# The first MLP product of a vision tower by seven quarter products, with ScalarE's copies placed anew

## The chip, the cores and the metric

The kernel runs on one core of one Trainium2 chip. The metric is the device time in microseconds of one execution; lower is better. All matrix products are in float32.

## What is computed

The reference is one tokenizer, one attention-like layer and one layer of eight experts. Cut to what matters:

```
h = (rfft of overlapping patches of x) @ tok_W.T              # 16384 tokens of 256
n = layernorm(layernorm(h)) * ln1_g + ln1_b
q, k, v = n @ Wq.T + bq, n @ Wk.T + bk, n @ Wv.T + bv
mem[t] = decay * mem[t-1] + k[t] * v[t]                       # along time
x = layernorm(h) + q * mem
h2 = layernorm(x) * ln2_g + ln2_b
a = relu(h2 @ W1.T + b1)                                      # 256 -> 1024: the first MLP product
h = h + x + (a @ W2.T + b2)                                   # 1024 -> 256
t = layernorm(h);  choose the top 2 of 8 experts from t @ router_w.T
out = h + t + sum over the two of weight * (gelu(t @ w1[e] + b1[e]) @ w2[e] + b2[e])
```

## The kernel before, in words

**Blocks.** The 16384 tokens are worked in 32 blocks of 512 (`NB`, `BLK`). A block lives in a `Block` object whose methods issue the steps. The main loop runs over `i` from 0 to 30 and works on three blocks in each turn: `new` (block i: embedding, norm, q/k/v, scan, residual), `mid` (block i-1: the MLP) and `old` (block i-2: routing and sending its rows to the experts). Between them lie the experts' tiles: 256 rows of one expert each, about four in a block, done by `Tile` objects. After the loop a tail finishes the last block and the tiles left.

**Order.** PE, ACT, DVE and SP run under a schedule written out by hand (`manual_schedule`): each of these queues holds its instructions in the order in which the Python code issues them, and an instruction whose input isn't there holds up all behind it. Many methods are generators, and a `next(...)` issues the part up to the next `yield`. Only GpSimd's (POOL's) queue is ordered by the framework.

**One turn, in the order of issue.** (1) `embed` (L383 on): 20 products of 256 columns in three parts. ScalarE copies the first two results to `ab` (L405); VectorE forms the tile rows `h` from `ab` and from PSUM (L402, L422) and their statistics (L263, L264); GpSimd raises them to a power (`Norm.factors`, L283 to L288); VectorE writes the normed rows `zz` (L292). (2) Between the parts of `embed`: `features2` of `mid`, four ScalarE copies that put the transposed rows together as `hT` (L332), and `rows` and `turn3` of `old` (L698 and a DMA transpose). (3) `sum_up` (L620, L621): `h` plus `z`, plus the offsets `b2` of the second MLP product. (4) A slot for one expert tile (`expert_halves`): ScalarE's two copies to `xT` (L995), TensorE's `enter` (L1002) with Gelu (L1010), and `leave` of the tile before it (L1019), then VectorE's `sums` (L1031 to L1038) and GpSimd's adds to the output (L1048). (5) The first MLP product, `mlp_in`, in eight parts m of 128 output features: TensorE in `feature_mm` (L339), then a Relu on ScalarE (L640). In between, at m = 1, `join3` (four ScalarE copies to `tokT`, L332) and `split1` (two ScalarE copies to `planes`, L318, and a DMA transpose of them to `turned`, L326); at m = 3 a second tile; at m = 4 `store`, four ScalarE operations (L683) and a DMA; at m = 5 the first half of `differences` for the next block, `features1` (four VectorE copies, L332) and `mix_tokens` (L508 to L511). (6) `logits` (L723) and `choose` (L747 on). (7) The q, k and v products, each already by seven products of quarters (`products`, L524 to L560): the 256 features and the 512 tokens are each cut in two. One of each pair of left-hand quarters is replaced by a sum prepared once (`wqkv_mix`), one of each pair of right-hand quarters by a sum made on the block (`s1`, `s2`, `s4`). Two more tiles stand between its rounds. (8) `scan` (L586 to L597), the second MLP product's first half (`mlp_out(0)`, L650, added to `h` at L657), `residual` (transposes at L608, added at L611, statistics, `factors_here`), `split2` (as `split1`, of the second norm, for `features2` of the next turn), and `mlp_out(1)` with `take`, a row of small VectorE operations that assigns the next tiles.

**Buffers that matter.** PSUM: three `tm` buffers in turn (embedding, `leave`, `mlp_out`, `residual`, `logits`), two `mm` buffers (`enter`, q/k/v), and three fixed banks `sums`. SBUF: one `turned`, one `planes`, five buffers for expert weights (641.5 KB each), six for a tile's rows `xh`, two `xT`.

The first six blocks (`EARLY`) turn their rows on TensorE instead of by DMA. The change adds `run` ahead of `Turn` and leaves the rest of what isn't shown below as it is.

Of the kernel before, what the change touches and what calls it, by code (L numbers as in the profile page):

```python
# [36 lines left out]
def vit_tower_kernel(  # L37
# [120 lines left out]
    nc.sync.dma_start(out=w1_sb, in_=w1.rearrange("(k p) h -> p k h", p=P))  # L158
    w2_sb = const.tile([P, KH, D], F32)
# [26 lines left out]
    for e in range(E + 1):  # L186
# [13 lines left out]
    none = const.tile([P, 2, RW], F32)  # L200
    nc.gpsimd.memset(none, 0.0)
    nc.gpsimd.iota(
        none[:, :, NUMBER : NUMBER + 1].bitcast(I32), pattern=[[1, 2]], base=NTOK, channel_multiplier=2
    )

# [5 lines left out]
    six = ctx.enter_context(tc.tile_pool(name="six", bufs=6))  # L211
    five = ctx.enter_context(tc.tile_pool(name="five", bufs=5))
    twelve = ctx.enter_context(tc.tile_pool(name="twelve", bufs=12))
    small = ctx.enter_context(tc.tile_pool(name="small", bufs=2))

# [25 lines left out]
    def mix_weights():  # L241

        w = wqkv_sb.rearrange("p w k (m q) -> p w k m q", q=P)
        t1, t2, t4 = [wqkv_mix[:, :, i, :] for i in range(3)]
        nc.vector.tensor_tensor(t1, w[:, :, 0, 1], w[:, :, 0, 0], ALU.subtract)
        nc.vector.tensor_tensor(t2, w[:, :, 1, 1], t1, ALU.subtract)
        nc.vector.tensor_tensor(t4, w[:, :, 1, 0], t2, ALU.subtract)
        nc.vector.tensor_tensor(w[:, :, 0, 1], w[:, :, 1, 1], w[:, :, 0, 1], ALU.subtract)

    def restore_weights():  # L250

        w = wqkv_sb.rearrange("p w k (m q) -> p w k m q", q=P)
        nc.vector.tensor_tensor(w[:, :, 0, 1], w[:, :, 1, 1], w[:, :, 0, 1], ALU.subtract)
# [57 lines left out]

    class Turn:


        def split(self, src):
            planes = one.tile([P, TT, 2 * D], U16, name="planes")
            for i, half in enumerate(halves(src)):
                nc.scalar.copy(planes[:, :, i * D : (i + 1) * D], half)  # L318
            self.start([planes.rearrange("p t d -> p (t d)")])

        def start(self, planes):
            self.turned = one.tile([P, TT, 2, KD, P], U16, name="turned")
# [5 lines left out]
        def join(self, dst, copy):  # L328
            for k in range(KD):
                to = dst[:, k, :].bitcast(U16).rearrange("p (t q i) -> p i t q", t=TT, i=2)  # L330
                for i in range(2):
                    copy(to[:, 1 - i], self.turned[:, :, i, k, :])  # L332

# [16 lines left out]
    class Block:  # L350
# [83 lines left out]

        def first_norm(self):
# [10 lines left out]
        def split1(self):  # L446
# [3 lines left out]
            self.turn.split(self.zz)  # L450
# [52 lines left out]
        def mix_tokens(self):  # L503

            room = one.tile([P, TT, 2 * D], U16, name="planes").rearrange("p t d -> p (t d)").bitcast(F32)
# [113 lines left out]
        def sum_up(self):  # L619
            nc.vector.tensor_tensor(self.h, self.h, self.z, ALU.add)  # L620
            nc.vector.tensor_tensor(self.h, self.h, mb2_sb.unsqueeze(1).to_broadcast([P, TT, D]), ALU.add)  # L621
# [7 lines left out]
        def features2(self):  # L629
# [4 lines left out]
            self.turn.join(self.hT, nc.scalar.copy)  # L634

# [74 lines left out]
        def join3(self, copy):  # L710
            self.tokT = one.tile([P, KD, BLK], F32, name="tokT")
            self.turn.join(self.tokT, copy)
# [19 lines left out]
        def choose(self):  # L732
# [7 lines left out]
            lg = small.tile(shape, F32, name="lg")  # L740
# [5 lines left out]
            turned = small.tile([P, TT, G], F32, name="turned_lg")  # L746
# [3 lines left out]
            key = small.tile(shape, F32, name="key")  # L750
# [40 lines left out]
        def place(self, at_once=True):  # L791
# [5 lines left out]
            before = small.tile([P, TT, E], F32, name="before")  # L797
# [153 lines left out]
    added = []  # L951

    class Tile:
# [6 lines left out]
        def load(self):  # L960
            t = self.t
            self.w = five.tile([P, NW], F32, name="w")
            if self.block.i < NS - 1:
                wrow = nc.sync.value_load(self.table[:, 0, t : t + 1], min_val=0, max_val=(E - 1) * P)
                nc.sync.dma_start(out=self.w, in_=wex[bass.ds(wrow, P), :])
# [5 lines left out]
            self.xh = six.tile([P, 2 * KD, S], U16, name="xh")  # L971
# [9 lines left out]

        def fetch(self):
            if self.block.i >= NS - 1:

# [73 lines left out]
    class Expert:  # L1058
# [10 lines left out]

        def fetch(self):  # L1070
            pass
# [51 lines left out]
    at = dict(load=0, fetch=0, turn=0, enter=0, leave=0, sums=0)  # L1123
# [8 lines left out]
    def expert_halves(fetch=True, sums=True, load=True, turn=True):  # L1132

        n = at["enter"]
        if load:
            advance("load", n + AHEAD)
        assert at["load"] >= min(n + 2, len(tiles))
        advance("turn", n + 1 + turn)
        advance("enter", n + 1)
        yield  # L1140
# [5 lines left out]

    def run(steps):
        for _ in steps:
            pass
# [8 lines left out]
    def slot_halves(known, load=True, sums=True):  # L1158

        if len(tiles) - at["enter"] > LEFT and at["enter"] + 2 <= known:  # L1160
            yield from expert_halves(load=load, sums=sums)

    def slot(known, load=True):
        run(slot_halves(known, load))
# [7 lines left out]
    with tc.manual_schedule(engines=MANUAL):  # L1172
# [3 lines left out]
        for i in range(NS):  # L1176
# [3 lines left out]
            old = blocks[i - 2] if i >= 2 else None  # L1180
            embed = new.embed()
            next(embed)
            if i > 1:
                mid.features2()
# [15 lines left out]
            if at["enter"]:  # L1200
                slot(known, load=False)
            for m in range(KH):
                if mid:
                    mid.mlp_in(m)
                if m == 1:
                    if old and i >= EARLY:
# [3 lines left out]
                    if at["enter"]:  # L1210
                        advance("load", at["enter"] + AHEAD - 1)
# [4 lines left out]
                if m == KH // 2 and old:  # L1216
                    if i < EARLY:
                        old.join3(nc.scalar.copy)
                    old.store()
# [241 lines left out]
```

## Time and profile before

| what | value |
|---|---|
| median of 3 runs | 2113.02 us (2112.82 to 2114.13) |
| the profiled execution, its own time | 2116.49 us |
| its span, first to last instruction | 2114.7 us |
| mean granted TensorE clock | 0.994 |
| embedding of block 7 starts / of the last block | 370.07 / 1853.01 us |
| first MLP product, 32 blocks (L339) | 451.7 us busy, x1024 instructions |
| ScalarE's Relu behind it (L640) | 167.0 us busy, x256 |

From 370.07 to 1853.01 the loop runs 24 blocks in 1482.9 us, 61.8 each. A float32 product is two instructions on TensorE in the trace.

A line of the page or of a list of groups names source line, engine, operation and tiles; then come the count and busy time. In a timeline a line begins with the start and the duration in us of a run of like instructions; a bracket at its end says how long the engine had idled before it, and for what. "PEld" is TensorE's weight load, "SPq" SP's queue.

### The profile page before, as it was taken

To read this page: it belongs to the slowest core of one execution; us is meant where nothing else is said; L and a number is where in the kernel's file an instruction comes from. 1 tells how busy PE (TensorE), PEld (TensorE's weight loads), DVE (VectorE), ACT (ScalarE), POOL (GpSimd) and SP (SyncE) were. 2 spreads that over 40 slices of the span, in tenths; PEclk is the share of its full clock that TensorE was granted. 3 is DMA by queue.
4 is the path that set the end of the run, shared out by engine and by line. 5 is a ranking of instruction groups with operands and counts; after the bars stand their busy time and mean duration, and the time that the engine had idled before them with its cause. 6 is when DMAs were issued, how large, how long until landed. Compare 5 with 4: busy or idle time off the path is not lost.

```text
span 2114.7 us, 30454 instructions
## 1 busy us (share of the span) xinstructions
PE 2077.4 (98%) x9042; PEld 1576.0 (75%) x9042; DVE 1674.8 (79%) x5179; ACT 1100.8 (52%) x1966; POOL 886.9 (42%) x768
## 2 busy tenths in 40 slices
PE   8999999999999999999999999999999999998999
PEld 5777677777777777777777777787777787676776
DVE  6778888888888888888888888888888888767445
ACT  2344455655545565554556555455665545543453
POOL 1032234444444444544444444444444444535444
PEclk9999999999999999999999999999999999999999
DMA  4031256766676676567667766766776567688653
GB/s 142 4 123 64 80 131 138 160 143 129 134 157 146 155 160 139 125 143 159 156 143 160 150 122 136 157 156 143 163 157 118 138 149 161 138 197 168 91 69 50
DMA packets 424519, 283.21 MB, mean 134 GB/s; under 512 B 355104, under 2 KB 391072, under 8 KB 420256
## 3 DMA queue, kind: packets, MB, share of 16 engines
q1 hardware_dynamic: 373424, 208.35, 42.5%
q0 software_dynamic: 49632, 67.39, 17.8%
q10 hardware_dynamic: 1296, 5.52, 0.8%
q8 instruction: 71, 1.16, 0.2%
q14 instruction: 96, 0.79, 0.1%
HBM read 118.36 MB, written 86.52 MB: 97 GB/s over the span
## 4 chain that ended last, share of the span: by engine, by line
PE 74%; DVE 11%; ACT 5%; DMA 5%; issue 2%; POOL 2%; SPq 1%; another core or an unknown queue 0%; ACTq 0%; DVEq 0%; POOLq 0%
PE tm L650 17%; PE sums L339 13%; PE tm L396 9%; PE sums L524 9%; PE mm L1002 8%; PE tm L1019 8%; DMA turned<-planes 3%; DVE st L263 2%; PE mm L540 1%; ACT planes L318 1%; ACT tokT L332 1%; PE tm L1098 1%; PE mm L1081 1%; PE mm L539 1%; SPq L326 1%
## 5 line engine op out<-in xcount | busy, mean ns | idle before, releaser
L1048 POOL DMA_INDIRECT out<-y,xg x226 | 369.2, 1634 | 432.7 <-DVE y L1038 220.2
L650 PE MATMUL tm<-w_sb,aT 128*128 128x256 f32 x2048 | 454.7, 380 | 0.0
L339 PE MATMUL sums<-hT,w_sb 128*128 128x512 f32 x1024 | 451.7, 593 | 1.3 <-ACT aT L640 1.3
L650 PEld LDWEIGHTS tm<-w_sb,aT 128*128 128x128 f32 x2048 | 386.7, 190 | 57.2 <-DVE z L611 4.8
L819 POOL DMA_INDIRECT xbuf<-row,to x248 | 257.1, 1037 | 294.3 <-DVE ks L560 170.5
L339 PEld LDWEIGHTS sums<-hT,w_sb 128*128 128x128 f32 x1024 | 193.4, 190 | 219.9 <-issue 201.0
L396 PE MATMUL tm<-wu,xv 128*128 128x256 f32 x1280 | 282.5, 379 | 0.0
L318 ACT COPY planes<-zz 128x1024 uint16<-128x1024 uint16 x100 | 99.3, 1041 | 342.0 <-DVE zz L292 342.0
L396 PEld LDWEIGHTS tm<-wu,xv 128*128 128x128 f32 x1280 | 242.7, 190 | 32.7
L1002 PE MATMUL mm<-xT,w 128*128 128x256 f32 x1048 | 252.5, 384 | 6.9 <-ACT xT L995 3.8
L1019 PE MATMUL tm<-w,ge 128*128 128x256 f32 x1048 | 253.4, 385 | 0.0
L1002 PEld LDWEIGHTS mm<-xT,w 128*128 128x128 f32 x1048 | 201.3, 193 | 49.9 <-issue 16.0
L1019 PEld LDWEIGHTS tm<-w,ge 128*128 128x128 f32 x1048 | 195.9, 191 | 31.4 <-issue 2.9
L640 ACT ACTIVATE aT<-sums,vec 128x512 f32<-128x512 f32 x256 | 167.0, 690 | 60.6 <-PE sums L339 59.3
L995 ACT COPY xT<-xh 128x512 uint16<-128x512 uint16 x262 | 182.1, 767 | 24.4 <-DMA xh<-xbuf 15.4
L283 POOL TENSOR_SCALAR rstd<-mv 128x4 f32<-128x4 f32 x62 | 42.0, 678 | 333.2 <-DVE mv L264 296.7
L1010 ACT ACTIVATE ge<-mm,w 128x256 f32<-128x256 f32 x262 | 109.9, 474 | 137.5 <-PE mm L1002 76.3
L1036 DVE TENSOR_TENSOR y<-tm,w 128x512 f32<-128x512 f32 x131 | 90.6, 691 | 97.9 <-PE tm L1019 86.6
L332 ACT COPY hT<-turned 128x512 uint16<-128x512 uint16 x100 | 66.2, 762 | 80.5 <-DMA turned<-planes 80.5
L263 DVE BATCH_NORM_STATS2 st<-h 128x6 f32<-128x256 f32 x256 | 104.8, 409 | 3.3
L332 ACT COPY tokT<-turned 128x512 uint16<-128x512 uint16 x116 | 76.5, 760 | 58.7 <-DMA turned<-row 58.7
L524 PE MATMUL sums<-hT,wqkv_sb 128*128 128x256 f32 x360 | 107.1, 379 | 0.0
(224 smaller groups left out, 3105.4 us busy)
## 6 DMA issues: line engine op xcount, KB each, us to landing
w<-in_wex SPq DMA_DIRECT2D x113, 641.5 KB
xb<-in_x SPq DMA_DIRECT2D x32, 1040.0 KB
out<-h SPq DMA_DIRECT2D x31, 512.0 KB
bank<-in_wex ACTq DMA_DIRECT2D x8, 641.5 KB
xbuf<-row,to POOLq DMA_INDIRECT x248
out<-y,xg POOLq DMA_INDIRECT x226
xh<-xbuf SPq DMA_TRANSPOSE x131
xg<-xbuf SPq DMA_DIRECT2D x131, 4.0 KB
```

What stands on the lines that cost most here:

```text
L263: nc.vector.bn_stats(self.st[:, t, :], src[:, t, :])
L332: copy(to[:, 1 - i], self.turned[:, :, i, k, :])
L339: nc.tensor.matmul(ps, lhsT=w[:, k, ts(m, P)], rhs=rhs[:, k, :], start=k == 0, stop=k == KD - 1)
L396: nc.tensor.matmul(ps[:, n, :], lhsT=xv[:, i, j, :], rhs=wu[:, i, j, :], start=j == 0, stop=j == J - 1)
L524: nc.tensor.matmul(g[:, n, :], lhsT=lhsT, rhs=rhs, start=False, stop=True, skip_group_check=True)
L640: nc.scalar.activation(self.aT[:, m, :], ps, AF.Relu, bias=vec[:, MB1 + m : MB1 + m + 1])
L650: last_product[0] = nc.tensor.matmul(ps[:, i, :], lhsT=self.aT[:, k, ts(u * 2 + i, P)], rhs=w2_sb[:, k, :], start=k == 0, stop=k == KH - 1,)
L819: write = nc.gpsimd.indirect_dma_start(out=xbuf, out_offset=bass.IndirectOffsetOnAxis(ap=self.to[:, c, t : t + 1], axis=0), in_=self.row[: ...
L995: nc.scalar.copy(halves[:, :, :, 1 - i], self.xh[:, i * KD : (i + 1) * KD, :])
L1002: nc.tensor.matmul(ps[:, m, :], lhsT=self.w[:, k * D + m * P : k * D + (m + 1) * P], rhs=self.xT[:, k, :], start=k == 0, stop=k == KD - 1,)
L1019: last_product[0] = nc.tensor.matmul(ps[:, c, :], lhsT=self.ge[:, k, ts(c, P)], rhs=w[:, (2 + k) * D : (3 + k) * D], start=k == 0, stop=k ...
L1048: add = nc.gpsimd.indirect_dma_start(out=out, out_offset=bass.IndirectOffsetOnAxis(ap=number[:, c, :], axis=0), in_=y[:, c, :], in_offset= ...
```

## The change

The diff has these parts.

- **The first MLP product** of block 6 and on (turn 7 and on) is made by `mlp_group` in place of `mlp_in`: four groups of 256 output features, each from seven products of quarters (128 features by 256 tokens) in four rounds of two, two, two and one. ScalarE copies partial sums from one PSUM place to another between the rounds, adds the bias, and does the Relu; VectorE joins the other half of the features (`other`), and a last ScalarE Relu works in place on it. Groups 0 to 2 go abreast, round by round; then comes a tile's `enter`, their last round, and group 3 around the tile's `leave` and `logits`. Group 3's last product and the four Relu in place are issued after the first of the q/k/v parts.
- **Sums of inputs**: `w1_mix` holds the sums of W1's quarters, made once at turn 6; `mix_normed` makes `s1`, `s2`, `s4` of `mid`'s tokens on VectorE, in the room of `kv`, after the first part of `embed`.
- **ScalarE's order**: `features2` and the copies of one tile's `xT` now stand ahead of the first part of `embed`, so ahead of `ab`; the `xT` copies of a further tile follow the slot's Gelu. `join3` is issued copy by copy around `split1` and the groups. `store` moves behind the scan.
- **Offsets**: adding `b2` moves from VectorE in `sum_up` to GpSimd (`add_offsets`), after `first_norm`.
- **VectorE's order**: a slot's `sums` are issued later, the first half of `differences` before the second tile's `leave`, the second half after the first q/k/v part; `logits` comes before the last round of group 3.
- **Room**: expert weights have four buffers instead of five and are loaded by a step of their own (`weigh`), one tile less ahead; `xh` has five instead of six; `split1` has a `turned_first` of its own; some small tiles have one buffer. After the loop W1 and Wqkv are restored and `w1_mix` serves as a weight buffer.

```diff
+    def whole_or_mixed(which):
+
+        for w, _ in which:
+            nc.vector.tensor_tensor(w[:, :, 0, 1], w[:, :, 1, 1], w[:, :, 0, 1], ALU.subtract)
+
+    def mix_weights(which):
+
+        for w, mixed in which:
+            t1, t2, t4 = [mixed[:, :, i, :] for i in range(3)]
+            nc.vector.tensor_tensor(t1, w[:, :, 0, 1], w[:, :, 0, 0], ALU.subtract)
+            nc.vector.tensor_tensor(t2, w[:, :, 1, 1], t1, ALU.subtract)
+            nc.vector.tensor_tensor(t4, w[:, :, 1, 0], t2, ALU.subtract)
+        whole_or_mixed(which)
...
+        def split(self, src, name="turned"):
+            run(self.split_steps(src, name))
+
+        def split_steps(self, src, name="turned"):
             planes = one.tile([P, TT, 2 * D], U16, name="planes")
             for i, half in enumerate(halves(src)):
                 nc.scalar.copy(planes[:, :, i * D : (i + 1) * D], half)
-            self.start([planes.rearrange("p t d -> p (t d)")])
-
-        def start(self, planes):
-            self.turned = one.tile([P, TT, 2, KD, P], U16, name="turned")
+                if i:
+                    self.start([planes.rearrange("p t d -> p (t d)")], name)
+                yield
+
+        def start(self, planes, name="turned"):
+            self.turned = one.tile([P, TT, 2, KD, P], U16, name=name)
             n = TT // len(planes)
             for j, plane in enumerate(planes):
                 to = self.turned[:, j * n : (j + 1) * n]
                 nc.sync.dma_start(out=to.rearrange("p t i k q -> p (t i k) q"), in_=plane, transpose=True)
 
         def join(self, dst, copy):
+            run(self.join_steps(dst, copy))
+
+        def join_steps(self, dst, copy):
             for k in range(KD):
                 to = dst[:, k, :].bitcast(U16).rearrange("p (t q i) -> p i t q", t=TT, i=2)
                 for i in range(2):
                     copy(to[:, 1 - i], self.turned[:, :, i, k, :])
+                    yield
...
+        def add_offsets(self):
+            nc.gpsimd.tensor_tensor(self.h, self.h, mb2_sb.unsqueeze(1).to_broadcast([P, TT, D]), ALU.add)
...
+        def mix_normed(self):
+            if self.i < EARLY:
+                return
+            self.mix_halves(one.tile([P, KD, BLK], F32, name="kv").rearrange("p k c -> p (k c)"))
+
+        def mix_halves(self, room):
+
             a, b = self.hT[:, 0, :], self.hT[:, 1, :]
             s1, s2, s4 = self.mix = [room[:, ts(i, HALF)] for i in range(3)]
...
         def sum_up(self):
             nc.vector.tensor_tensor(self.h, self.h, self.z, ALU.add)
-            nc.vector.tensor_tensor(self.h, self.h, mb2_sb.unsqueeze(1).to_broadcast([P, TT, D]), ALU.add)
...
+        def mlp_group(self, j):
+
+            if j == 0:
+                self.aT = one.tile([P, KH, BLK], F32, name="aT")
+            w11, w12, w21, w22 = [w1_sb[:, k, ts(2 * j + m, P)] for k in range(2) for m in range(2)]
+            t1, t2, t4 = [w1_mix[:, j, i, :] for i in range(3)]
+            a, b = self.hT[:, 0, :], self.hT[:, 1, :]
+            s1, s2, s4 = self.mix
+            g = sums[j % 3].rearrange("p (n c) -> p n c", n=2)
+            one_, other = self.aT[:, 2 * j, :], self.aT[:, 2 * j + 1, :]
+            bias = [vec[:, MB1 + 2 * j + m : MB1 + 2 * j + m + 1] for m in range(2)]
+
+            def product(dst, lhsT, rhs, start=False):
+                nc.tensor.matmul(dst, lhsT=lhsT, rhs=rhs, start=start, stop=True, skip_group_check=True)
+
+            pool, name = (p_tm, "tm") if j == 2 else (p_mm, "mm")
+            ps = pool.tile([P, 2, HALF], F32, name=name)
+            product(ps[:, 1, :], t1, s1, True)
+            product(ps[:, 0, :], w11, a[:, :HALF], True)
+            p5 = three.tile([P, HALF], F32, name="p5")
+            nc.scalar.activation(p5, ps[:, 1, :], AF.Identity, bias=bias[1])
+            nc.scalar.copy(g[:, 1, :], ps[:, 0, :])
+            yield
+            product(g[:, 1, :], t2, s2)
+            product(ps[:, 0, :], w21, b[:, :HALF])
+            nc.scalar.activation(one_[:, :HALF], ps[:, 0, :], AF.Relu, bias=bias[0])
+            nc.scalar.copy(g[:, 0, :], g[:, 1, :])
+            yield
+            product(g[:, 1, :], w12, a[:, HALF:])
+            product(g[:, 0, :], w22, s4)
+            other = other.rearrange("p (n c) -> p n c", n=2)
+            nc.vector.tensor_tensor(other, g, p5.unsqueeze(1).to_broadcast([P, 2, HALF]), ALU.add)
+            yield
+            product(g[:, 1, :], t4, b[:, HALF:])
+            nc.scalar.activation(one_[:, HALF:], g[:, 1, :], AF.Relu, bias=bias[0])
+            yield
+            nc.scalar.activation(other, other, AF.Relu)
+            yield
 
         def mlp_in(self, m):
...
+    def room_of_weights():
+
+        if spare and next(turns) % 5 == 3:
+            return spare[0]
+        return four.tile([P, NW], F32, name="w")
...
+        def weigh(self):
+            t = self.t
+            if self.block.i < NS - 1:
+                self.w = room_of_weights()
+                wrow = nc.sync.value_load(self.table[:, 0, t : t + 1], min_val=0, max_val=(E - 1) * P)
+                nc.sync.dma_start(out=self.w, in_=wex[bass.ds(wrow, P), :])
...
+    def expert_halves(fetch=True, sums=True, load=True, turn=True, further=False):
 
         n = at["enter"]
         if load:
+            advance("weigh", n + AHEAD - (not spare))
             advance("load", n + AHEAD)
         assert at["load"] >= min(n + 2, len(tiles))
         advance("turn", n + 1 + turn)
         advance("enter", n + 1)
+        if further:
+            advance("turn", min(n + 3, at["load"]))
...
+            seven = i > EARLY
             embed = new.embed()
+            if seven:
+                mid.features2()
+                advance("turn", min(at["enter"] + 2, at["load"]))
             next(embed)
-            if i > 1:
+            if seven:
+                mid.mix_normed()
+            elif i > 1:
                 mid.features2()
             if old:
...
+                slot(known, load=False, further=seven, sums=not seven)
+            ahead = blocks[i + 1].differences(xs.pop(i + 1))
+            groups = [mid.mlp_group(j) for j in range(KH // 2)] if seven else []
+            rest = groups[-1] if seven else iter(())
+            if seven:
+                for _ in range(3):
+                    for group in groups[:3]:
+                        next(group)
+                tokens = old.join3_steps(nc.scalar.copy)
+                next(tokens)
+                new.split1()
+                next(tokens)
+                advance("weigh", at["enter"] + AHEAD - 2)
+                advance("load", at["enter"] + AHEAD - 1)
+                tile_steps = slot_halves(known, sums=False)
+                next(tile_steps, None)
+                for group in groups[:3]:
+                    next(group)
+                next(rest)
+                advance("sums", at["leave"])
+                run(tokens)
+                next(ahead)
+                run(tile_steps)
+                next(rest)
+                new.features1()
+                new.mix_tokens()
+                old.logits()
+                next(rest)
+                advance("sums", at["leave"])
+            for m in range(0 if seven else KH):
...
             later = iter(())
             if i:
                 qkv = new.qkv()
                 if old:
-                    old.logits()
                     old.choose()
+                next(qkv)
+                run(chain(rest, *groups[:3]))
                 if i >= EARLY:
-                    next(ahead)
-                next(qkv)
+                    run(ahead)
                 next(qkv)
                 tile_steps = slot_halves(known, sums=False)
...
                 new.first_norm()
+                new.add_offsets()
                 for m in range(KD):
                     new.scan(m)
+                if old:
+                    old.store()
                 if EARLY <= i < NB - 2:
                     xs[i + 2] = load_x(i + 2)
                 mid.mlp_out(0)
...
             new.residual()
             if 0 < i < EARLY:
-                next(ahead)
+                run(ahead)
             run(later)
             if old:
                 old.scatter(4, last_product[0])
             if i == 0:
-                mix_weights()
+                mix_weights(QUARTERS[:1])
             else:
                 new.split2()
+            if i == EARLY:
+                mix_weights(QUARTERS[1:])
```

## The prediction

> **What bounds the kernel now.** I read the page first, then the busy times of one steady block by stage, then that block's timelines of TensorE, ScalarE, VectorE and GpSimd. From the page:
>
> ```profile
> span 2114.7 us, 30454 instructions
> PE 2077.4 (98%) x9042; PEld 1576.0 (75%) x9042; DVE 1674.8 (79%) x5179; ACT 1100.8 (52%) x1966; POOL 886.9 (42%) x768
> ```
>
> TensorE is busy all the time. The block from 1047.77 to 1109.44, cut at the first MLP product, the first q/k/v product, the second MLP product and the end (columns: PE, PEld, DVE, ACT, POOL busy, then clock and DMA):
>
> ```profile
> 1047.77:1059.86 12.09, 12.09 (x58) 10.64 (x57) 11.31 (x48) 6.99 (x10) 4.57 (x5) 1.00 0.76 142
> 1059.86:1077.71 17.85, 17.85 (x65) 9.30 (x64) 11.66 (x29) 14.73 (x26) 7.57 (x6) 1.00 0.56 104
> 1047.77:1109.44 61.67, 61.35 (x269) 47.00 (x268) 51.17 (x161) 34.58 (x63) 27.68 (x23) 1.00 0.66 147
> ```
>
> PE lacks 0.32 us in the block, and it is in one place:
>
> ```profile
> 1047.77 8.80 PE L396 MATMUL tm<-wu,xv 128*128 128x256 f32 x40
> 1056.40 1.89 PE L1002 MATMUL mm<-xT,w 128*128 128x256 f32 x8
> 1059.86 7.03 PE L339 MATMUL sums<-hT,w_sb 128*128 128x512 f32 x16
> 1078.73 0.70 PE L540 MATMUL mm<-planes,wqkv_mix 128*128 128x256 f32 x2 [0.32 <-DVE planes L508]
> ```
>
> So two limits nearly coincide: TensorE's work, and a chain of latencies that ends in that 0.32 us wait for `s1`. ScalarE's part of the chain, in its queue order:
>
> ```profile
> 1051.42 0.59 ACT L405 COPY ab<-tm 128x512 f32<-128x512 f32 x1 [1.86 <-PE tm L396]
> 1055.26 2.65 ACT L332 COPY hT<-turned 128x512 uint16<-128x512 uint16 x4 [3.25 <-DMA turned<-planes]
> 1057.77 1.98 ACT L698 COPY row<-tok 128x1024 uint16<-128x1024 uint16 x2
> 1059.65 1.39 ACT L995 COPY xT<-xh 128x512 uint16<-128x512 uint16 x2
> 1060.90 0.83 ACT L1010 ACTIVATE ge<-mm,w 128x256 f32<-128x256 f32 x2
> 1068.73 1.98 ACT L318 COPY planes<-zz 128x1024 uint16<-128x1024 uint16 x2
> ```
>
> `ab` is copied at 1051.42, long before the turned rows land (1055.26). VectorE and GpSimd take over:
>
> ```profile
> 1055.90 0.76 DVE L402 SCALAR_TENSOR_TENSOR h<-ab 128x256 f32<-128x256 f32 x2
> 1060.95 1.20 DVE L620 TENSOR_TENSOR h<-h,z 128x1024 f32<-128x1024 f32 x1
> 1065.25 1.38 DVE L292 TENSOR_SCALAR zz<-h,mv,rstd 128x256 f32<-128x256 f32 x4 [1.84 <-POOL rstd L288]
> 1078.25 0.43 DVE L508 TENSOR_TENSOR planes<-hT 128x256 f32<-128x256 f32 x1
> ```
>
> ```profile
> 1052.71 0.23 POOL L283 TENSOR_SCALAR rstd<-mv 128x4 f32<-128x4 f32 x1
> 1061.12 1.11 POOL L283 TENSOR_SCALAR rstd<-mv 128x4 f32<-128x4 f32 x1 [6.93 <-DVE mv L264]
> 1062.30 1.16 POOL L285 TENSOR_SCALAR rstd<-mv 128x4 f32<-128x4 f32 x1
> ```
>
> **What the skill says.** (1) "ScalarE: Activation LUTs", What ACT_TABLE_LOAD costs: an activation takes 186 ns + 0.833 ns an element, 93 ns more for a pointer bias. That is 492 ns at 256; the trace has 482 (L527). (2) "SBUF — State Buffer", Who interferes with whom: a VectorE instruction with two SBUF inputs and a GpSimd instruction that reads SBUF exclude each other for a whole instruction. The trace agrees: L283 takes 0.23 us alone and 1.11 beside L620. (3) "GPSIMD Engine Reference", Elementwise: 4497 ns for a two-input add of 2048, so by estimate 2.3 us for 1024; the trace has no such GpSimd add.
>
> **The change, part by part.** Times from here are from the start of a block's embedding products, t = 0 = 1047.77. Blocks 7 to 30 take the new path: 24 of them.
>
> *Products.* Before, 32 instructions of 512 columns take two stretches of 6.9 us: 13.8. After, 4 groups of 7 products, two instructions each, are 56 of 256 columns; 40 such take 8.65 (L396 to L1002), so 0.216 each and 12.1. Saved: **1.73 us** a block, 41.5 in all, if TensorE stays fed.
>
> *New ScalarE work.* A group has p5 0.48, two copies of 0.36, two half Relu of 0.48 and a Relu in place over 512 (0.6 back to back): 2.8; four are 11.1 against eight Relu of 0.69, 5.5. So 34.6 + 5.6 = 40.2 of some 62 us: not the bound as a sum.
>
> *New VectorE work.* Four joins of 0.69 (L560's size), four sums of `mix_normed` in 1.47 (1078.25 to 1079.72), less the offset add of 1.22 (L621): +3.0, 54.2 a block; not the bound as a sum either.
>
> *Order at the block's head.* This decides. `features2` and a tile's `xT` copies now stand **ahead of `ab`** in ScalarE's queue. Before: four hT copies from 7.49 (the DMA's landing) to 10.00. The landing doesn't move: its source is `zz` of `split2`, which VectorE finishes 0.24 before t = 0 because both follow the end of the second MLP product's first half. So after: hT to 10.00, xT 1.25 (1059.65 to 1060.90) to 11.25, `ab` 0.59 to 11.84, first `h<-ab` at 11.90. Before it was 8.13: **3.77 late**. Behind `ab` wait, on VectorE, the whole embedding norm, and on TensorE the tile's `leave`, whose PSUM room `ab` frees (from 10.4 to 11.9: TensorE stalls, but has room, below).
>
> *`mix_normed`* stands between `h<-ab` and the other embedding sums: **+1.47** on the same chain. From `h<-ab` to the last statistics was 5.13 (1055.90 to 1061.03).
>
> *Offset add to GpSimd.* L285 took 1.16 for want of the port while L621 ran; alone I price it like L283's 0.23. The GpSimd part was 4.13 (1061.12 to 1065.25): **-0.9**. Unknown is the add's own cost at its new place, beside the scan. Low bound 0, if it runs behind the scatters and `out` DMAs, when VectorE reads only one SBUF input; high bound 2.3, if it locks out a scan. Not below nothing: the 0.9 is counted. I take 0.
>
> *`zz` to the first q/k/v product.* `zz` starts at 11.90 + 5.13 + 1.47 + 0.09 + 3.23 = 21.8 and ends at 23.2. Before, planes started at 20.96, not at `zz`'s end at 18.86, since `join3` stood in front for 2.1; with the join split ScalarE is free when `zz` is there. Planes at 23.25: **+2.29**. From there to the product with `s1` 10.0 passed (1068.73 to 1078.73: planes, SP's issue, landing, four copies, `s1`), and nothing of that changes. So `s1`'s product is at 33.25 instead of 30.96. TensorE's work ahead of it, 27.9, is done with all group waits by some 32.5 in a walk along the queues (a group's copies, 0.82 a pair of operations, keep behind its 0.86 of products), so the chain sets the time.
>
> *From there to the block's end.* Before: 30.71. New on TensorE: the last quarter product of group 3, 0.43. It waits some 0.5 for that group's join, which stands behind `mix_tokens` on VectorE. Behind it VectorE has a tile's `sums` (1.7), `choose` (2.9) and the second half of `differences` (3.3): the scan, 14.6 after the `s1` product before, starts at about 15.9, and the residual's first add some 1.2 later than before in all (those 0.43 and 0.5 within). **+1.2**. ScalarE's four Relu in place (2.4) fit: the second round of q/k/v copies ends as TensorE leaves the tile.
>
> *Moved without cost.* `store` (four activations of 0.61 and a DMA) goes into ScalarE's 13.66 us of idling before `split2`'s planes; on SP it holds back the next load of x, used a block later. If that cover were gone, at most 2.1 on the chain. The expert weights, loaded with one buffer less, have SP's queue behind them: a late buffer would delay transposes; I take 0. Mixed W1 costs 4 operations of 0.69 once, on a chain: +2.
>
> *Sum.* 2.29 + 1.2 = **+3.5 us** a block, 84 for 24, and 2: 86. The profiled execution took 2116.5 (span 2114.7); 2116.5 + 86 = 2202.5. It stands 3.5 above the median of 2113.0, so **2199** for the median.
>
> **Rivals.** *A, as forecast*: head chain late, 2199. Its lower end is without xT's 1.25 and half of the 1.2: 3.5 - 1.9 = 1.6 a block, 2154; its upper end takes 1 us of lock: 2223. *B, faster*: the copies and joins stay hidden and TensorE's saving shows: 2113.0 - 41.5 = 2071.5. For it: 98% busy now. Against: the 0.32 us wait shows the chain without slack. It decides only if the head's chain gets 3.5 + 1.7 = 5.2 us shorter than in my walk, that is, if the turned rows land by about 2.3 rather than 7.5. *C, worse*: GpSimd's add locks out a scan in each block, or SP waits for a weight buffer: 2.3 more, 2199 + 55 = 2254. For it: the lock is seen at L283. Against: GpSimd's queue puts the add behind DMAs until the scan is over. *D, the change does less than it says*, as many cycles for quarters as for halves: excluded by 0.216 against 0.43 for twice the columns.
>
> **Chances.** A 0.70, C 0.20, B 0.08, and 0.02 for a chain that happens to cancel the saving. About 0.2% (4 us) is what can be told from no change. Faster 0.08, same 0.02, slower 0.90. The range goes from 2150 (leaving out B and the same) to 2254.
>
> **What would show it.** In the profile after: `ab` copied behind hT and xT, some 12 after the embedding starts, with the next `h<-ab` waiting on ScalarE; a TensorE gap before L1019 and before the q/k/v products; a period of about 65.2 instead of 61.7; TensorE near 93%; L285 at 0.3. I am wrong if hT's copies start soon after `ab`'s products end, or if TensorE has no gap before the q/k/v products.

## The result, and the profile after

The changed kernel takes 2173.97 us (median; 2170.49 to 2181.74) against 2112.92 for the kernel before on the same chip: 1.0297 times as long [1.0275, 1.0319]. The forecast was 2199 with a range of 2150 to 2254: the direction is right, and the loss is 61 us where 86 were forecast. The profiled execution took 2172.28 us, with a span of 2170.5. From its page, the lines that answer to those shown of before:

```profile
span 2170.5 us, 32402 instructions
PE 2075.3 (96%) x9618; PEld 1671.4 (77%) x9618; DVE 1752.8 (81%) x5344; ACT 1203.7 (55%) x2350; POOL 963.1 (44%) x800
```

TensorE has 576 instructions more and hardly less busy time (2075.3 us against 2077.4). The turn that I follow begins at t = 0 = 1015.50. The busy times by stage, up to the first product with `s1` and up to the turn's end (columns as before):

```profile
1015.50:1047.32 31.82, 29.79 (x145) 23.92 (x144) 24.56 (x81) 22.20 (x42) 11.77 (x10) 1.00 0.54 105
...
1015.50:1078.76 63.26, 61.09 (x293) 50.87 (x292) 53.78 (x168) 38.76 (x78) 30.72 (x24) 1.00 0.66 143
```

Of the 2.17 us in which PE isn't busy, 2.03 lie in the first half. PE's timeline shows where:

```profile
1015.50 8.80 PE L414 MATMUL tm<-wu,xv 128*128 128x256 f32 x40
1024.13 1.89 PE L1082 MATMUL mm<-xT,w 128*128 128x256 f32 x8
1027.53 1.99 PE L1099 MATMUL tm<-w,ge 128*128 128x256 f32 x8 [1.51 <-ACT ab L423]
...
1031.57 0.70 PE L676 MATMUL tm<-kv,w_mix 128*128 128x256 f32 x2 [0.28 <-DVE h L420]
...
1045.92 0.70 PE L676 MATMUL sums<-hT,w_sb 128*128 128x256 f32 x2 [0.23 <-ACT sums L689]
...
1047.32 0.59 PE L568 MATMUL mm<-planes,wqkv_mix 128*128 128x256 f32 x2
```

The tile's `leave` (L1099) waits 1.51 us for `ab`. The product with `s1` (L568) has no bracket, so there is no wait: `s1` is there when TensorE comes to it. ScalarE and VectorE explain both:

```profile
1023.17 2.63 ACT L349 COPY hT<-turned 128x512 uint16<-128x512 uint16 x4 [5.70 <-DMA turned<-planes]
1025.67 1.37 ACT L1075 COPY xT<-xh 128x512 uint16<-128x512 uint16 x2
1026.90 0.57 ACT L423 COPY ab<-tm 128x512 f32<-128x512 f32 x1
...
1038.82 1.99 ACT L330 COPY planes<-zz 128x1024 uint16<-128x1024 uint16 x2 [2.05 <-DVE shift L449]
```

```profile
1037.35 1.38 DVE L297 TENSOR_SCALAR zz<-h,mv,rstd 128x256 f32<-128x256 f32 x4 [2.13 <-POOL rstd L293]
...
1045.13 1.47 DVE L349 COPY hT<-turned_first 128x512 uint16<-128x512 uint16 x4 [0.30 <-DMA turned_first<-planes]
1046.70 0.42 DVE L536 TENSOR_TENSOR planes<-hT 128x256 f32<-128x256 f32 x1
```

ScalarE stands idle for 5.70 us at the head of the turn, for most of it with `ab`'s products done, because the hT copies ahead of `ab` wait for a transpose. From planes to hT it is 6.31 us (1038.82 to 1045.13); in the block shown of before the same step took 7.94 (1068.73 to 1076.67).

**Where the 55.8 us of span are.** By the starts of the embedding products, turn 7 begins at 382.02 instead of 370.07 (+12.0); the 24 turns to the last block take 1529.6 instead of 1482.9 (+46.7); the rest takes 258.9 instead of 261.7 (-2.8).

**Work and waits of a turn.** I cut twelve turns (15 to 26) into TensorE's work, which is the count of each kind of instruction times the median spacing of its starts (the sixteen short ones of `logits` together 0.57), and what is left over:

| kernel | turn | work | left over |
|---|---|---|---|
| before | 61.4 | 60.6 | 0.8 |
| after | 63.5 | 59.0 | 4.5 |

So seven products do save 1.6 us a turn. Of what is left over after, 2.1 stands ahead of the tiles' `leave` (L1099; 0.3 before) and 2.3 among the rounds of the groups (L676). This counts each start's delay, also that which PE's modelled ends hide.

**The early turns** don't use the new path, and yet lose 12 us. In a turn of that part, with VectorE, GpSimd and TensorE:

```profile
192.07 0.97 POOL L888 DMA_INDIRECT xbuf<-row,to  x1 [0.30 <-issue]
...
192.83 3.68 DVE L615 TENSOR_TENSOR_SCAN ks<-vec,carry,kv 128x512 f32<-128x512 f32 x1
193.07 2.35 POOL L454 TENSOR_TENSOR h<-h,mb_sb 128x1024 f32<-128x1024 f32 x1
...
197.72 0.98 PE L636 MATMUL tm<-ident,ret 128*128 128x128 f32 x7 [1.68 <-DVE ret L625]
```

The scan, 1.28 us for the other half of the same turn, takes 3.68 while GpSimd adds the offsets (the lock that rival C named), and TensorE waits for what follows it. GpSimd comes to the add right behind the four scatters of the rows (L888). In turns 5 and 6, which lose 6.2 of the 12 us, the add comes later and shuts out the product behind the scan instead, `ret` (L625, 3.4 us). In the later turns, here that at 1015.50, a tile's two adds to the output stand in between on GpSimd's queue. Three lines of GpSimd and one of VectorE:

```profile
1065.73 1.61 POOL L1128 DMA_INDIRECT out<-y,xg  x1 [0.30 <-issue]
1067.65 1.56 POOL L1128 DMA_INDIRECT out<-y,xg  x1 [0.30 <-issue]
1068.67 2.93 POOL L454 TENSOR_TENSOR h<-h,mb_sb 128x1024 f32<-128x1024 f32 x1
...
1067.88 1.08 DVE L625 TENSOR_TENSOR ret<-ret,ks 128x512 f32<-128x512 f32 x1
```

The last VectorE instruction that this add could block, the second `ret`, starts 0.8 us ahead of the add and takes its usual time. There the add does no harm, by those 0.8 us; in no turn from 7 to 30 is the lead much smaller (0.78 at the least).

### The profile page after: what moved, and what is told of

The parts are those of the page before. It is cut to its first block, busy times and chain, and to the rows that moved or that the text cites. A ratio compares the mean times of both kernels' runs of the same rounds, so it can differ in the third digit from the quotient of the medians.

```text
span 2170.5 us, 32402 instructions
## 1 busy us (share of the span) xinstructions
PE 2075.3 (96%) x9618; PEld 1671.4 (77%) x9618; DVE 1752.8 (81%) x5344; ACT 1203.7 (55%) x2350; POOL 963.1 (44%) x800
## 4 chain that ended last, share of the span: by engine, by line
PE 44%; DVE 27%; DMA 11%; ACT 7%; issue 5%; POOL 4%; POOLq 0%; DVEq 0%; SPq 0%; ACTq 0%
PE tm L716 11%; PE sums L552 8%; PE mm L1082 6%; PE sums L357 6%; DMA turned<-planes 4%; DMA turned_first<-planes 4%; PE tm L1099 4%; DVE st L268 4%; DVE h L420 3%; ACT planes L330 3%; PE tm L414 2%; DVE zz L297 2%; ACT hT L349 2%; DMA out<-y,xg 2%; POOL rstd L293 2%
## 5 line engine op out<-in xcount | busy, mean ns | idle before, releaser
L1128 POOL DMA_INDIRECT out<-y,xg x226 | 387.5, 1715 | 441.8 <-DVE y L1118 217.4
L888 POOL DMA_INDIRECT xbuf<-row,to x248 | 262.1, 1057 | 169.2 <-DVE ks L588 88.9
L1099 PE MATMUL tm<-w,ge 128*128 128x256 f32 x1008 | 248.2, 390 | 36.2 <-ACT ab L423 36.2
L1082 PE MATMUL mm<-xT,w 128*128 128x256 f32 x1008 | 241.9, 383 | 6.6 <-ACT xT L1075 4.5
L1099 PEld LDWEIGHTS tm<-w,ge 128*128 128x128 f32 x1008 | 187.8, 192 | 74.7 <-ACT ab L423 45.5
L1082 PEld LDWEIGHTS mm<-xT,w 128*128 128x128 f32 x1008 | 192.8, 192 | 37.1 <-ACT xT L1075 5.6
L357 PE MATMUL sums<-hT,w_sb 128*128 128x512 f32 x256 | 112.8, 592 | 0.0
L389 DVE TENSOR_TENSOR xv<-xb 128x512 f32<-128x512 f32 x160 | 104.2, 684 | 4.1 <-DMA xb<-in_x 4.1
L454 POOL TENSOR_TENSOR h<-h,mb_sb 128x1024 f32<-128x1024 f32 x32 | 90.7, 2835 | 23.9 <-ACT z L459 23.8
L297 DVE TENSOR_SCALAR zz<-h,mv,rstd 128x256 f32<-128x256 f32 x128 | 44.2, 409 | 67.2 <-POOL rstd L293 67.2
```

The costliest lines, as they stand in the source:

```text
L357: nc.tensor.matmul(ps, lhsT=w[:, k, ts(m, P)], rhs=rhs[:, k, :], start=k == 0, stop=k == KD - 1)
L888: write = nc.gpsimd.indirect_dma_start(out=xbuf, out_offset=bass.IndirectOffsetOnAxis(ap=self.to[:, c, t : t + 1], axis=0), in_=self.row[: ...
L1082: nc.tensor.matmul(ps[:, m, :], lhsT=self.w[:, k * D + m * P : k * D + (m + 1) * P], rhs=self.xT[:, k, :], start=k == 0, stop=k == KD - 1,)
L1099: last_product[0] = nc.tensor.matmul(ps[:, c, :], lhsT=self.ge[:, k, ts(c, P)], rhs=w[:, (2 + k) * D : (3 + k) * D], start=k == 0, stop=k ...
L1128: add = nc.gpsimd.indirect_dma_start(out=out, out_offset=bass.IndirectOffsetOnAxis(ap=number[:, c, :], axis=0), in_=y[:, c, :], in_offset= ...
```

## The experiments

The theory: `ab` behind the transposed rows delays the turn's head, and GpSimd's add blocks the scan in the early turns. The rivals: the add, or a denser VectorE, causes the loss in the later turns too; or the groups' rounds can't be hidden at all, wherever `ab` stands. Waits of TensorE are shown from 700 to 1800, some 17 to 18 turns; the columns are the total, how often, and the longest, in us. For the kernel after:

```profile
PE tm L1099 <- ACT ab L423: 27.2, 18, 2.8
PE tm L676 <- DVE h L420: 5.1, 18, 0.3
PE sums L676 <- ACT sums L689: 3.9, 17, 0.2
PE sums L676 <- DVE aT L694: 2.3, 14, 0.2
```

**`ab` first, on the kernel after.**

```diff
+            next(embed)
             if seven:
                 mid.features2()
                 advance("turn", min(at["enter"] + 2, at["load"]))
-            next(embed)
-            if seven:
                 mid.mix_normed()
```

> The changed kernel with one order undone: ab is copied before hT and the tile's xT on ScalarE. Theory A (the head's order makes the loss): VectorE's first h<-ab returns from 11.9 to about 8.1 us after the embedding starts, the sums of mix_normed then wait for hT until 10.0, zz ends some 2.6 us sooner, TensorE loses its 1.5 us wait for ab; the period falls from 63.4 to about 61.2 us and the time to about 2120 (2110 to 2130). Rival B (the seven products cost it by themselves, through ScalarE's copies and the rounds' waits): the time stays above 2160.

Measured: 2136.31 us, 1.0114 [1.0081, 1.0146], somewhat above the 2110 to 2130 that were expected. The median turn falls from 63.4 to 61.35, that of before being 61.4; the early turns keep their loss (turn 7 at 380.88). The wait for `ab` is gone, but another stands in its place:

```profile
PE mm L676 <- ACT ge L1090: 17.4, 16, 2.2
PE tm L636 <- DVE ret L625: 6.4, 3, 2.2
PE sums L676 <- ACT sums L689: 4.7, 18, 0.3
```

The place of `ab` is worth 2.0 us in the median turn. Now the first group waits for the Gelu of the tile, which stands behind hT and xT on ScalarE, and in three turns of this stretch GpSimd's add, issued earlier now, blocks `ret` (L625); together with the early turns this is what keeps the time above the forecast.

**`ab` late, on the kernel before.**

```diff
+            if i > EARLY:
+                mid.features2()
+                advance("turn", min(at["enter"] + 2, at["load"]))
             next(embed)
-            if i > 1:
+            if 1 < i <= EARLY:
                 mid.features2()
```

> The kernel before with that one order put in, from turn 7 on: hT and one tile's xT are copied ahead of ab; all else as before, products of halves too. Theory A: h<-ab comes 3.3 us late, of which the slack of some 1.5 to 2.1 us ahead of split1's planes takes a part; the period grows by 1.3 to 2 us and the time from 2113 to 2145 to 2160. Rival B: no more than 2120, since no seven products are in it.

Measured: 2150.89 us, 1.0182 [1.0156, 1.0208], as expected; the median turn is 63.0. Its timelines of ScalarE and TensorE repeat those of after:

```profile
1010.53 2.64 ACT L332 COPY hT<-turned 128x512 uint16<-128x512 uint16 x4 [5.65 <-DMA turned<-planes]
...
1014.90 1.99 PE L1019 MATMUL tm<-w,ge 128*128 128x256 f32 x8 [1.27 <-ACT ab L405]
```

With no other part of the change, this order costs 1.6 us in the median turn. Taken both ways, out of after and into before, the place of `ab` is shown to be the main loss of the later turns.

**The offsets back on VectorE, on the kernel after.**

```diff
         def add_offsets(self):
-            nc.gpsimd.tensor_tensor(self.h, self.h, mb2_sb.unsqueeze(1).to_broadcast([P, TT, D]), ALU.add)
+            pass
...
             nc.vector.tensor_tensor(self.h, self.h, self.z, ALU.add)
+            nc.vector.tensor_tensor(self.h, self.h, mb2_sb.unsqueeze(1).to_broadcast([P, TT, D]), ALU.add)
```

> The changed kernel with the offsets added on VectorE again, behind h plus z, as before. Theory A: GpSimd's second rstd operation waits for the port again (1.16 instead of 0.19 us), zz and all behind it come 0.9 to 1.0 us later, and the time rises by some 20 us to about 2195. Rival C (GpSimd's 2.9 us add locks out VectorE or holds up the scatters): the time falls, to 2160 or less.

Measured: 2181.17 us, 1.032 [1.0296, 1.0343], between the two expectations, because it does two things. The early loss is gone: turn 7 begins at 368.86, 13.2 earlier than after. But the later turns become 0.9 longer (median 64.3), and TensorE's waits say why:

```profile
PE tm L1100 <- ACT ab L423: 25.3, 18, 2.7
PE sums L677 <- DVE aT L695: 14.2, 27, 0.8
```

VectorE, with 1.22 us more, joins the groups later (2.3 us of such waits in the kernel after, 14.2 now). So the add on GpSimd is a loss of 13 in the early turns and a gain of 0.9 a turn in the later ones, and the add isn't what makes the later turns slow.

**`ab` first, and the xT copies later.** From the first experiment; the copies for two slots are issued ahead of the groups' third round and with the second tile, no longer at the head.

```diff
-                advance("turn", min(at["enter"] + 2, at["load"]))
...
-                slot(known, load=False, further=seven, sums=not seven)
+                slot(known, load=False, turn=not seven, sums=not seven)
...
-                for _ in range(3):
+                for n in range(3):
+                    if n == 2:
+                        advance("turn", min(at["enter"] + 1, at["load"]))
```

> As the kernel with ab first, and besides the xT copies of the head and of the slot (four copies, 2.6 us of ScalarE) are taken out of ScalarE's queue ahead of the first rounds: one tile's xT is copied after the second round, when ScalarE has nothing of the groups to do; the other tile's with the second tile. If ScalarE's backlog holds up the groups' rounds once ab is no longer late (theory A goes on): another 0.8 to 1.3 us a block, 2085 to 2100. If only ab's place matters: the same as with ab first alone, within 5 us.

Measured: 2183.42 us, 1.0334 [1.0309, 1.0359]: missed by far. The wait for the Gelu is gone (0.2 us in all from 700 to 1800), and some turns take 60.8, although a new wait of 1.0 us a turn for a group's partial sums (L684, 16.9 in all) stands in them. But 15 of the 24 take over 64. In a long one:

```profile
1066.51 2.91 POOL L454 TENSOR_TENSOR h<-h,mb_sb 128x1024 f32<-128x1024 f32 x1
1066.86 3.48 DVE L625 TENSOR_TENSOR ret<-ret,ks 128x512 f32<-128x512 f32 x1
...
1070.40 0.98 PE L636 MATMUL tm<-ident,ret 128*128 128x128 f32 x7 [2.13 <-DVE ret L625]
...
1071.22 3.44 PE L1099 MATMUL tm<-w,ge 128*128 128x256 f32 x8
```

The add now meets `ret`, which takes 3.48 us instead of 1.09. TensorE waits 2.13, and then its next products take 3.44 us instead of 1.9: the busy times of the stretch behind the wait give a granted clock of 0.50.

```profile
1071.50:1073.00 1.50, 1.50 (x5) 1.23 (x4) 1.43 (x5) 0.00 (x0) 0.98 (x1) 0.50 0.85 219
```

The 0.8 us of luck in the kernel after is used up as soon as anything ahead moves: here the add starts 0.35 us ahead of `ret`. A block of 2.4 us costs most turns about 4 (64.6 to 65.6 against 60.8).

**Only the add to GpSimd, on the kernel before.** Here `add_offsets` is called after `first_norm`, as in the change, and the line on VectorE is removed.

> The kernel before with only the offset add moved to GpSimd, behind the first norm. If GpSimd's add shuts VectorE's scan out: the early turns (0 to 6) grow by 1.4 us each, some 10 to 12 in all, and of the later ones those in which the add falls on the scan's end; against that GpSimd's second rstd operation is 0.9 us shorter, which a turn bound by TensorE shows little of: 2112 to 2130 in all. If the add is only the gain that the prediction counted (0.9 us a turn on a chain without slack): 2095 to 2108.

Measured: 2200.53 us, 1.0406 [1.038, 1.0433]. The lock is as expected, the size far above it: turn 7 begins at 381.53 (before 370.07), which is the early loss of after by itself, and the later turns have a median of 65.2. The first two lines are VectorE and GpSimd, the third TensorE:

```profile
949.42 4.28 DVE L590 TENSOR_TENSOR_SCAN ks<-vec,carry,kv 128x512 f32<-128x512 f32 x1
949.70 2.91 POOL L436 TENSOR_TENSOR h<-h,mb_sb 128x1024 f32<-128x1024 f32 x1
...
954.91 1.75 PE L611 MATMUL tm<-ident,ret 128*128 128x128 f32 x7 [2.66 <-DVE ret L600]
```

The expectation took only some of the later turns to be hit, and all 24 are: the scan in 19 of them, `ret` in five. And it priced the wait and not the half clock behind it. In five of the 24 no lower clock follows the wait of 2.7 us; these take 63.7 to 64.1, the other nineteen 64.8 to 65.6.

**`ab` first, and the offsets on VectorE in its gap ahead of `mix_normed`.** From the first experiment.

```diff
         def add_offsets(self):
-            nc.gpsimd.tensor_tensor(self.h, self.h, mb2_sb.unsqueeze(1).to_broadcast([P, TT, D]), ALU.add)
+            nc.vector.tensor_tensor(self.h, self.h, mb2_sb.unsqueeze(1).to_broadcast([P, TT, D]), ALU.add)
...
+                mid.add_offsets()
                 mid.mix_normed()
```

In the early turns it is called behind `sum_up`.

> The changed kernel with ab copied first, and with the offsets added on VectorE instead of GpSimd: from turn 7 on between the first h<-ab and the sums of mix_normed, where VectorE waits 1.2 us for hT; before that, behind h plus z. Theory A2 (two causes: the head's order, and GpSimd's 2.9 us add that locks VectorE out of a scan in the early turns and, with ab first, in some later ones): the early turns take 48.4 and 50.2 us again, no turn of 68 to 70 us is left but the last, the typical turn stays near 61.3, and the time is about 2100 (2092 to 2110), below the kernel before. If the add on GpSimd is harmless and the rest of the loss lies in the products: 2125 to 2140, as with ab first alone.

Measured: 2116.35 us, 1.0016 [1.0007, 1.0025], somewhat above what was expected. Turn 7 begins at 369.5, no turn shows the lock any more, and the median turn is 61.2. With both faults undone, the change ends where the kernel before stood: the 1.6 us saved in products go for the most part into the wait for the Gelu, the rest into short waits among the rounds.

```profile
PE mm L676 <- ACT ge L1090: 16.6, 18, 2.2
PE sums L676 <- ACT sums L689: 4.7, 18, 0.3
```

**The same with the xT copies placed later**, as in the fourth edit, and those of the second tile behind it:

```diff
-                tile_steps = slot_halves(known, sums=False)
+                tile_steps = slot_halves(known, sums=False, turn=False)
...
                 run(tile_steps)
                 next(rest)
+                advance("turn", min(at["enter"] + 1, at["load"]))
                 new.features1()
```

> As the one before, and ScalarE's xT copies leave the way of the groups: those of the head go behind the second round, those of the slot and the second tile behind group 3's second round, where ScalarE idles some 2 us. Theory: TensorE loses its wait for the Gelu ahead of the second group (1.0 us) and for group 3's copy (1.3 us in the kernel with late turns); the turn falls to 60.2 to 60.8 us against 59.9 of work, the time to about 2080 (2070 to 2093). If ScalarE's backlog isn't what is left: no better than the one before, 2095 to 2110.

Measured: 2108.03 us, 0.9976 [0.9966, 0.9985], the only kernel here that beats the one before, and by far less than expected. The median turn is 61.0. TensorE's waits are nearly all gone:

```profile
PE sums L676 <- ACT sums L689: 4.1, 18, 0.2
PE mm L676 <- ACT ge L1090: 1.8, 3, 1.0
PE mm L568 <- DVE planes L536: 1.5, 3, 0.8
```

In the twelve turns 15 to 26 the work is again 59.0 (the expectation had taken 59.9), and 2.0 is left over where before had 0.8, mostly in delays of 0.1 to 0.4 us at the rounds of the groups. Its last turn takes 69.9 (before 67.3). There TensorE waits for expert weights, which have one buffer less since the change:

```profile
1809.10 2.96 PE L1082 MATMUL mm<-xT,w 128*128 128x256 f32 x8 [2.04 <-DMA w<-in_wex]
```

The kernel after has the same wait in that turn (2.06). That the missing buffer causes it wasn't tried alone.

**The slots' sums later, on the kernel before**, to see whether the outputs' adds slow the transpose:

```diff
-                slot(known, load=False)
+                run(slot_halves(known, load=False, sums=i <= EARLY))
...
-                    slot(known)
+                    run(slot_halves(known, sums=i <= EARLY))
...
                         new.mix_tokens()
+                        if i > EARLY:
+                            advance("sums", at["leave"])
```

> The kernel before with the sums of the two tiles around the first MLP product issued later, behind mix_tokens, from turn 7 on, so that their adds into the output do not run beside split1's transpose. If those adds slow the transpose: from the start of split1's planes to the first hT copy 6.3 to 6.6 us instead of 7.7, as in the changed kernel. If not: 7.7. The time is not the question; 2105 to 2135, as VectorE's later sums may hold up the scan.

Measured, in one execution: 2256.01 us, far outside the expectation. The adds, now later, stand ahead of `ex` on GpSimd's queue (L769, a step of `choose`), VectorE waits for it ahead of the joins of q, k and v, and TensorE waits for these, 56.4 us from 700 to 1800:

```profile
DVE share L774 <- POOL ex L769: 57.2, 16, 4.7
PE sums L524 <- DVE ks L560: 56.4, 16, 4.4
```

The question has its answer all the same. From planes to hT:

```profile
999.46 1.98 ACT L318 COPY planes<-zz 128x1024 uint16<-128x1024 uint16 x2
1001.46 1.99 SPq L326 DMA_TRANSPOSE turned<-planes  x1
1005.79 1.46 DVE L332 COPY hT<-turned 128x512 uint16<-128x512 uint16 x4 [5.66 <-DMA turned<-planes]
```

That is 6.33 us, with no indirect add to the output (L1048) beside the transpose; 22 of the 24 turns lie between 6.26 and 6.48. In the block of before, where it takes 7.94, two begin there, at 1068.35 and 1070.31. Over all 24 turns of before it takes 6.7 to 9.4: 6.7 to 7.0 in the seven turns whose first add begins 0.9 us or more ahead of planes, 7.5 and more in the other seventeen. In the kernel after, the first begins at 1042.21, 3.4 us after planes, and the step takes 6.31.

## Why the prediction was right, and where it was off

**Right: the order at the head.** Forecast and measured after t = 0: `ab` done at 11.84 and 11.97; `zz` starts at 21.8 and 21.85; planes start at 23.25 and 23.32. L290 takes 0.19 us where 0.23 was priced, and 1.16 in the median with the offsets back on VectorE. The first two experiments show the cause both ways. TensorE is 96% busy by the page, not 93, and the mean turn is 63.7 instead of 65.2.

**Off: "From there to the product with `s1` 10.0 passed ... and nothing of that changes."** Something did: the slots' sums, which the change issues later, had their adds to the output beside the transpose. It lands 1.6 us sooner relative to planes, and the product with `s1` comes at 31.82, not 33.25: +0.86 against before (30.96), where +2.29 was forecast.

**Off: "TensorE stalls, but has room, below".** With the chain shorter, TensorE had no room. It reaches that product at 31.82 by its own work and its own waits, 1.5 of them for `ab`. The walk gave 32.5 for this, so the term was there and was thought hidden. The second sign of being wrong that it named, "if TensorE has no gap before the q/k/v products", came true: it was the other of two nearly equal limits that ended last. The loss at the head was foreseen, the way by which it reaches the turn's end only in half.

**Smaller: "From there to the block's end", +1.2.** Measured: 63.26 - 31.82 = 31.44 against 30.71, +0.73. Head and rest make about +1.6 in this turn and 1.94 in the mean, 46.7 in all, where 84 was forecast.

**Off: the offset add, "I take 0".** It cost 12 us in turns 0 to 6, which the prediction didn't walk through at all: its cover was scatters and `out` DMAs. In turns 0 to 4 no tile leaves yet (the first add to the output is at 300.3 us), so the second half of that cover is missing; in turns 5 and 6 it is there and ends too soon. The price was right (2.35 us measured, high bound 2.3), and rival C named the mechanism. In the later turns the choice was right for the kernel as built, by 0.8 us. The Trainium skill, "SBUF — State Buffer", Who interferes with whom, gives the rule that the runs confirm: the scan and `ret`, each with two SBUF inputs, stand blocked beside a GpSimd add (3.68 us instead of 1.28, 3.48 instead of 1.09).

**Off: mixed W1, +2.** With the offsets back on VectorE (third experiment) turn 6 takes 62.6 us, as before (62.7). So the mix costs nothing measurable, and turn 6's 2.9 after are the add too.

**Right: the products.** 1.73 us saved a turn by forecast, 1.6 by the count of work. Rival B was wrong not on this but on "stay hidden": even with `ab` first and no lock, short waits at the rounds take most of it back. Of the 41.5 us promised, the best version here keeps some 5.

In sum: turns 0 to 6 +12.0 (forecast 2), later turns +46.7 (84), tail -2.8 (0). Errors of opposite sign made the forecast nearer than its terms were; that part is luck.

## What to carry to other kernels

An instruction that waits for a DMA must not stand ahead of one that frees PSUM or starts a chain on the same in-order queue: here that one exchange cost 1.6 us in the median turn of one kernel and 2.0 in the other, as much as the new algorithm saves (1.6) or more. When two limits nearly coincide, walk both to the end and let neither be "room" for the other. An addition moved to an idle engine has to be checked against the port lock in every phase of the program, and with the margin in us, since the next edit shifts it.

## What the hardware showed beyond expectation

**Gaps and the clock.** In all ten traces the granted clock changes only at the borders of a grid of 3.41 us, and only between full and half. I took TensorE's idle time in every such window at full clock between 300 and 1900 us. Of 4485 windows with up to 1.60 us of it none was followed by a window at half clock; of 33 with 1.60 to 2.02 fifteen were; all 66 with more were. A wait that a border cuts in two can therefore pass unpunished, as five of the 2.7 us do in the kernel with only the add moved. The products behind a wait (3.44 instead of 1.9 us) show what half clock costs: some 1.5 us more. The Trainium skill, "TensorE: Matmul & The Clock Gate", HAM oscillation, states a limit of about 3.4 us of idling; here some 2 us within one window were enough. This is a count over traces, with PE's modelled ends; no run varied the gap alone.

**Lock sizes.** Beside GpSimd's add of 1024 elements (2.35 us at the least) a scan takes 3.26 to 4.29 us (alone 1.28), a two-input product 2.96 to 3.51 (alone 1.09).

**A transpose beside adds to memory.** From planes to hT a transpose takes 7.6 us in the median of the kernel before, with two indirect adds to the output around its start, and 6.3 in the eighth experiment, with none.
